# Entry to the ternary convolution: another order of buffers, five for attention outputs, one for transformed rows, and half 1's scales and chain ahead of half 0's transform

## The chip, the cores and the metric

The kernel runs on one core of a Trainium2 chip. The metric is the device time of one execution in microseconds (us), as the median of several runs. The engines named below are TensorE (PE, matrix multiply), VectorE (DVE), ScalarE (ACT), GpSimd (POOL) and SyncE (SP, which here only issues transfers). Each engine works through its own instructions in their order and waits for the others by semaphores.

## The reference

Four layers follow each other on an image batch x of shape (4, 256, 64, 64), each as x = x + layer(groupnorm(x)) with 32 groups. They are an axial attention, a ternary 3x3 convolution, a block of binary convolutions and a convolution with generated weights. The change lies where the first gives way to the second.

```python
def _L0_conv_ref(x, w_qkv, ...):      # axial attention along one image axis
    ...
    sim = jax.nn.softmax(sim, axis=3)
    attn = jnp.einsum('ngij,ngcj->ngci', sim, v)
    attn_e = jnp.einsum('ngij,cij->ngci', sim, v_emb)
    out = jnp.concatenate([attn, attn_e], axis=-1)
    out = out.reshape(N, 2 * OUT_C, W)
    out = _bn(out, bn3_gamma, bn3_beta, axes=(0, 2), ch_axis=1)
    out = out.reshape(B, H, OUT_C, 2, W).sum(axis=-2)
    return out.transpose(0, 2, 1, 3)

def _L1_conv_ref(x, weight, alpha, bias):
    w_t = _ternize_ste(weight, THRESHOLD) * alpha
    out = jax.lax.conv_general_dilated(x, w_t, window_strides=(1, 1), padding=[(1, 1), (1, 1)], ...)
    return out + bias[None, :, None, None]

x = x + _L0_conv_ref(_gn(x), ...)
x = x + _L1_conv_ref(_gn(x), L1_conv_weight, L1_conv_alpha, L1_conv_bias)
x = x + _L2_conv_ref(_gn(x), ...)
x = x + _L3_conv_ref(_gn(x), ...)
```

The batch norm at the end of the attention needs the mean and variance over the whole batch, so the attention's outputs are stored first and scaled afterwards, when the next layer loads them. The group norm at the start of the convolution needs the sums of one whole image.

## The kernel before, in words

**The end of the attention.** It works in eight units, one for each image b and each half th of the 256 channels (half 0 of all four images, then half 1). For a unit, the softmax numbers of the tile pt are multiplied with the values (matmul on L945, eight pieces k) and with the embedded values (matmul on L970). DVE scales each piece out of PSUM into an SBUF tile: o0 (L954) for the first kind, o1 (L977, two pieces to a tile) for the second. The tile's statistics are taken (L959, L984), and ACT's queue issues its store to the tensors at_d in memory (L960, L985). The scale rb is copied from PSUM by ACT on L938. The tiles o0 and o1 have two buffers each.

**The convolution** lies in the function from_scores, in one with-block that opens its pools on L1227. An image is cut into four quarters q of 16 rows, and each quarter lies in two halves t of 128 channels. These steps are made of it:

- load(b, t, q), L1258: makes the row tile dx from the input x (the load is the helper's L145) and the two attention outputs, a1 (two loads on L1270, scaled by ACT on L1273, added by DVE on L1275) and a0 (a load of L145, multiplied and added by DVE on L1278, which also yields the sum). ACT squares the result into a junk tile for the sum of squares (L1256). The scales come from value_norm(t, two), L786, which ends the attention's batch norm for a half; before the change it is called for half 0 earlier, and for half 1 inside load(0, 1, 0).
- norm(b, ts), L1283: from the sums of an image's half to the group norm's factors: a chain of small operations on DVE (L1105 to L1110, L1292, L117 to L128 of the helpers, L1297 to L1300), three small matmuls (L115, L125, L126) and a square root on ACT.
- transform(b, t, q), L1303: ACT writes the normed rows into a padded tile (L1316), DVE makes the transformed rows dv of them (L1318, L1322, L1323), ACT casts dv into dh (L1328) and DVE takes the rest dl = dv - dh (L1329).
- chunk(b, q, co), L1334: 48 matmuls (L1351) of dh and dl of both halves with the weights d_u, for output half co; then the bias and the sums (L1366 to L1370), the addition to dx (L1375), another square, and stores to x2_d and, for co = 1, to z_d by POOL's queue (L1380, L1382).

The weights d_u are loaded by load_weights (L1246). The first chunk takes all products of half 0 before those of half 1 (by_tile). The driver at the end of the block loads five quarters ahead of the chunk at work and transforms one quarter ahead.

**What sets order and place.** The program is written to a scheduler that gives each engine an instruction order from the written order and its priorities (a with-block tc.high_priority() puts its contents ahead). The pools are laid out one after another in the order in which they are opened, over memory that the attention's tiles use as well. An instruction that writes into memory waits until the earlier tile on that memory was last read. In before the pools for the sums (tag st in the pool s), for the junk (in the pool o), for half 1's first row tile, for d_u1 and for half 1's dv lie over the attention's tile pt, which is read until the last matmul of L970.

**The next layer**, of binary convolutions, starts by loading x2_d (L1538) and its weights e_k (L1495) through SP's queue. ACT takes signs into the padded tile e_pad (L1549), DVE transforms them into e_tr (L1436), and PE multiplies them on L1447. Before these, the norm of the last image is ended and one small matmul (pbad) counts bad values.

Of the kernel before, what the change touches and what calls it, by code (L numbers as in the profile page):

```python
# [9 lines left out]
F32 = mybir.dt.float32  # L10
F32R = mybir.dt.float32r
BF16 = mybir.dt.bfloat16
# [6 lines left out]
P = 128  # L19
B = 4  # L20
C = 256
HW = 4096
# [19 lines left out]
def network(ctx: ExitStack, tc, x, wqkv, relm, relt, relw, relv, counts, masks, vecs, rowv, ab, w1, l2w1, l2w2, l3w, mats, out):  # L42
# [45 lines left out]
    def pool(stack, name, bufs=1, space=None, side=None):  # L88
        kw = {"space": space} if space is not None else {}
        return stack.enter_context(tc.tile_pool(name=name, bufs=bufs, side=side, reuse_waits="tile", **kw))  # L90
# [3 lines left out]
    def fresh(base):  # L94
        uid[0] += 1
        return f"{base}_{uid[0]}"
# [45 lines left out]
    def load_shuffled(dst, src, t):  # L142

        rows = src.rearrange("(two i) f -> i two f", two=2)[64 * t : 64 * t + 64]
        nc.sync.dma_start(out=dst, in_=rows)  # L145
# [20 lines left out]
    with ExitStack() as ph:  # L166
# [9 lines left out]
        pst = pool(ph, "a_pst", 1, PSUM)  # L176
# [102 lines left out]
        for b in range(B):  # L279
            xs, gm, rs = ready  # L280
# [129 lines left out]
    with ExitStack() as ph:  # L410
# [3 lines left out]
        op = pool(ph, "b_o", 2)  # L414
# [22 lines left out]
        for t in range(2):  # L437
            v = small(sp, [P, 2])
# [196 lines left out]
        for b in range(B):  # L635
            for gp in range(GP):
                j = 4 * b + gp // 2
                if j == 2 and gp % 2 == 0:
                    load_sums()
                q = qs[j]  # L640
# [103 lines left out]
    def from_scores(general, keep):  # L744
# [41 lines left out]
        def value_norm(th, two, psp, tag):  # L786


            mv3 = small(keep, [P, 2])
            nc.vector.bn_aggr(mv3, st3[:, th, two].rearrange("p k s -> p (k s)"))  # L790
            var, gam = mv3[:, 1:2], vec[:, V_BN3G + 2 * th + two : V_BN3G + 2 * th + two + 1]
            if two == 0:

                sv = s1[:, 2 + th : 3 + th]
                nc.vector.tensor_tensor(var, var, sv, ALU.mult)
                nc.vector.tensor_tensor(var, var, sv, ALU.mult)
                g = small(keep, [P, 1])
                nc.vector.tensor_tensor(g, gam, sv, ALU.mult)
                gam = g
            prm = small(keep, [P, 2])  # L800
            r = inv_std(keep, var, BN_EPS, [P, 1])
            nc.vector.tensor_tensor(prm[:, 0:1], r, gam, ALU.mult)
            nc.vector.tensor_tensor(prm[:, 1:2], mv3[:, 0:1], prm[:, 0:1], ALU.mult)
            beta = vec[:, V_BN3B + 2 * th + two : V_BN3B + 2 * th + two + 1]
            nc.vector.tensor_tensor(prm[:, 1:2], beta, prm[:, 1:2], ALU.subtract)
            ps = psp.tile([P, 2], F32, name=f"pprm{th}{two}", tag=tag)
            nc.tensor.matmul(ps, lhsT=mt[:, M_SHUF, :], rhs=prm, start=True, stop=True)
            res = small(keep, [P, 2])
            nc.vector.tensor_copy(res, ps)
            return res  # L810
# [415 lines left out]

        with ExitStack() as ph:  # L1227
            ps_ = {
                k: pool(ph, f"d_{k}", {"a": 3, "o": 2}.get(k, 1))
                for k in "x2 x3 a x4 x5 x0 x6 p0 v0 h00 l00 u0 u1 x1 o s v1 h10 l10 h11 l11 x7 x8 x9 p1 x10 x11 h01 l01".split()  # L1230
            }
            ap_, op, sp = ps_["a"], ps_["o"], ps_["s"]
            wide = pool(ph, "d_ps3", 1, PSUM)
# [3 lines left out]

            pads = [ps_[f"p{t}"].tile([P, 18, 66], F32, name=f"d_pad{t}", tag="pad") for t in range(2)]
            u = [ps_[f"u{t}"].tile([P, 3, 4, C], F32R, name=f"d_u{t}", tag="u") for t in range(2)]
            for t in range(2):  # L1240
                nc.vector.memset(pads[t][:, :, 0], 0.0)
                nc.vector.memset(pads[t][:, :, 65], 0.0)

            def load_weights(t):
                for dx in range(3):
                    nc.sync.dma_start(out=u[t][:, dx].bitcast(F32), in_=u1_d[:, t, dx])  # L1246
# [3 lines left out]
            def row_of(b, t, q):  # L1250
                xs[b, t, q] = ps_[f"x{2 * ((4 * b + q) % 6) + t}"].tile([P, HW // 4], F32, name=f"dx_{b}_{t}_{q}", tag="x")
                return xs[b, t, q]

            def square(src, out):
                junk = op.tile([P, HW // 4], BF16, name=fresh("dj"), tag="j", bufs=1)
                nc.scalar.activation(junk, src, AF.Square, accum_out=out)  # L1256

            def load(b, t, q):  # L1258

                if (b, t) not in sums:  # L1260
                    sums[b, t] = sp.tile([P, 4, 2], F32, name=f"dst_{b}_{t}", tag=f"st{t}", bufs=2)
                xt = row_of(b, t, q)
                load_shuffled(xt, x[b][:, bass.ts(q, HW // 4)], t)
                if b == 0 and t == 1 and q == 0:
                    for two in range(2):
                        prs[t, two] = value_norm(t, two, pst, "pst")
                a = ap_.tile([P, HW // 4], F32, name=f"a1_{b}_{t}_{q}", tag="a")
                for two in range(2):
                    src = at_d[1][b][t * P + 64 * two : t * P + 64 * two + 64].rearrange("i (k f) -> i k f", k=4)
                    nc.sync.dma_start(  # L1270
                        out=a[two:P:2].rearrange("p (k f) -> p k f", k=4), in_=src[:, :, bass.ts(q, 256)]
                    )
                nc.scalar.activation(a, a, AF.Copy, scale=prs[t, 1][:, 0:1])  # L1273
                xv = xt.rearrange("p (n k i) -> p n k i", k=4, i=16)
                nc.vector.tensor_tensor(xv, a.rearrange("p (k n i) -> p n k i", k=4, i=16), xv, ALU.add)  # L1275
                a = ap_.tile([P, HW // 4], F32, name=f"a0_{b}_{t}_{q}", tag="a")
                load_shuffled(a, at_d[0][b][bass.ts(t, P), bass.ts(q, HW // 4)], 0)
                nc.vector.scalar_tensor_tensor(  # L1278
                    xt, a, prs[t, 0][:, 0:1], xt, ALU.mult, ALU.add, accum_out=sums[b, t][:, q, 0:1]
                )  # L1280
                square(xt, sums[b, t][:, q, 1:2])
# [21 lines left out]
            def transform(b, t, q):  # L1303


                nb, ra = norms[b, t]
                pad = pads[t]
                if q in (0, 3):
                    nc.vector.memset(pad[:, 0 if q == 0 else 17, :], 0.0)
                parts = [(xs[b, t, q].rearrange("p (h w) -> p h w", w=64), slice(1, 17))]  # L1310
                if q > 0:
                    parts.append((xs[b, t, q - 1][:, 15 * 64 :].rearrange("p (h w) -> p h w", w=64), slice(0, 1)))
                if q < 3:
                    parts.append((xs[b, t, q + 1][:, 0:64].rearrange("p (h w) -> p h w", w=64), slice(17, 18)))
                for src, rows in parts:
                    nc.scalar.activation(pad[:, rows, 1:65], src, AF.Identity, bias=nb, scale=ra)  # L1316
                v = ps_[f"v{t}"].tile([P, 4, 8, 66], F32, name=f"dv_{b}_{t}_{q}", tag="v")
                nc.vector.tensor_tensor(  # L1318
                    v[:, 0:4:3].rearrange("p k q w -> p q k w"), pad[:, 0:16].rearrange("p (q k) w -> p q k w", k=2),
                    pad[:, 2:18].rearrange("p (q k) w -> p q k w", k=2), ALU.subtract,  # L1320
                )
                nc.vector.tensor_tensor(v[:, 1], pad[:, 1:17:2], pad[:, 2:18:2], ALU.add)  # L1322
                nc.vector.tensor_tensor(v[:, 2], pad[:, 2:18:2], pad[:, 1:17:2], ALU.subtract)  # L1323
                hi, lo = (
                    ps_[f"{k}{(4 * b + q) % 2}{t}"].tile([P, 4, 8, 66], F32R, name=f"d{k}_{b}_{t}_{q}", tag="tr")
                    for k in "hl"
                )
                nc.scalar.copy(hi, v)  # L1328
                nc.vector.tensor_tensor(lo, v, hi, ALU.subtract)  # L1329
                vs[b, t, q] = hi, lo  # L1330
# [59 lines left out]
            for q in range(4):  # L1390
                load(0, 0, q)
            load_weights(0)
            with tc.high_priority():
                norm(0, slice(0, 1))
            transform(0, 0, 0)
            for q in range(4):
                load(0, 1, q)
            load_weights(1)
            norm(0, slice(1, 2))
            transform(0, 1, 0)  # L1400
            for t in range(2):
                load(1, t, 0)
            for b in range(B):
                for q in range(4):
                    nxt = (b, q + 1) if q < 3 else (b + 1, 0)
                    far = divmod(4 * b + q + 5, 4)
                    for co in range(2):
                        if nxt[0] < B:
                            transform(nxt[0], co, nxt[1])
                        chunk(b, q, co, b == q == co == 0)  # L1410
                        if far[0] < B:
                            load(far[0], co, far[1])
                    if far[0] < B and far[1] == 3:
                        norm(far[0], slice(0, 2))
# [472 lines left out]
```

## Time and profile before

| | us |
|---|---|
| three runs | 2746.36, 2769.91, 2764.95 |
| median | 2764.95 |
| profiled execution | 2755.02 |
| its span | 2753.1 |
| granted clock of TensorE in it, mean | 0.936 of full speed |
| busy in the span: PE, DVE, ACT, POOL | 2399.8, 1978.8, 1202.4, 105.2 |
| last matmul of the attention (L970) ends at | 1463.1 |
| first matmul of the convolution (L1351) | 1489.81 |
| last matmul of the convolution ends at | 1890.9 |
| first matmul of the next layer (L1447) | 1906.59 |

A table by stretch gives busy time of each engine between two times of the span. A list of waits gives, for an engine and a line, how long it stood idle just before an instruction of that line and what ended the wait. A time line gives runs of equal instructions of one engine with the start, the busy time, the line, the operation, and in brackets the idle time before and what ended it. In names, the buffer numbers are left out: dx stands for all row tiles, a for both kinds of attention outputs, sm for small tiles.

### The profile page before, as it was taken

To read this page: it belongs to the slowest core of one execution; us is meant where nothing else is said; L and a number is where in the kernel's file an instruction comes from. 1 tells how busy PE (TensorE), PEld (TensorE's weight loads), DVE (VectorE), ACT (ScalarE), POOL (GpSimd) and SP (SyncE) were. 2 spreads that over 40 slices of the span, in tenths; PEclk is the share of its full clock that TensorE was granted. 3 is DMA by queue.
4 is the path that set the end of the run, shared out by engine and by line. 5 is a ranking of instruction groups with operands and counts; after the bars stand their busy time and mean duration, and the time that the engine had idled before them with its cause. 6 is when DMAs were issued, how large, how long until landed. Compare 5 with 4: busy or idle time off the path is not lost. (4 is left out here: it accounts for less than half of the span.)

```text
span 2753.1 us, 78131 instructions
## 1 busy us (share of the span) xinstructions
PE 2399.8 (87%) x34632; PEld 1582.9 (57%) x34632; DVE 1978.8 (72%) x3372; ACT 1202.4 (44%) x1984; POOL 105.2 (4%) x201
## 2 busy tenths in 40 slices
PE   7999788888998788888773999997979859999998
PEld 4666555656666566667663777775545424444443
DVE  6665788878675466666567999885878877867742
ACT  3555245545555644454444665553458411110100
POOL 0000100000001000000000000000000000000000
PEclk9999899999999899988986999998989979999999
DMA  6866366656656877777777655415347742424110
GB/s 234 269 197 193 92 185 178 162 162 188 160 148 146 238 260 243 263 246 250 250 234 237 211 191 195 159 67 191 127 146 261 279 157 92 144 101 138 46 44 34
DMA packets 287995, 489.86 MB, mean 178 GB/s; under 512 B 32736, under 2 KB 149088, under 8 KB 274848
## 3 DMA queue, kind: packets, MB, share of 16 engines
q1 hardware_dynamic: 224992, 359.52, 42.9%
q10 hardware_dynamic: 48256, 58.73, 6.2%
q0 software_dynamic: 14400, 66.53, 6.2%
q8 instruction: 273, 4.47, 0.7%
q14 instruction: 74, 0.61, 0.1%
HBM read 281.46 MB, written 203.23 MB: 176 GB/s over the span
## 5 line engine op out<-in xcount | busy, mean ns | idle before, releaser
L1066 PE MATMUL gc<-gtr,g_u 128*128 128x512 f32 x1152 | 504.4, 600 | 13.6 <-DVE pc_o L1459 6.9
L1066 PEld LDWEIGHTS gc<-gtr,g_u 128*128 128x128 f32 x1152 | 219.6, 192 | 290.1 <-issue 270.8
L512 DVE STREAM_TRANSPOSE t<-pd 128x1024 f32<-128x1024 f32 x256 | 304.5, 1228 | 93.4 <-PE pd L505 92.3
L505 PE MATMUL pd<-rm,qb 64*32 64x256 f32 x8192 | 312.6, 396 | 44.2 <-DVE t L512 34.7
L1447 PE MATMUL pc<-e_tr,e_k 128*64 128x512 bf16 x2304 | 264.3, 390 | 24.3 <-DVE e_tr L1436 17.9
L532 ACT ACTIVATE o<-pq 128x512 f32<-128x512 f32 x256 | 150.4, 593 | 274.2 <-PE pq L526 270.1
L505 PEld LDWEIGHTS pd<-rm,qb 64*32 64x32 f32 x8192 | 172.9, 109 | 138.1 <-DVE t L512 60.5
L1351 PE MATMUL dc<-dh,d_u 128*128 128x512 f32 x768 | 229.6, 407 | 15.6 <-ACT dh L1328 15.6
L907 ACT ACTIVATE pt<-pt,sm 128x512 f32<-128x512 f32 x256 | 162.6, 709 | 177.0 <-DVE pt L877 136.6
L1351 PE MATMUL dc<-dl,d_u 128*128 128x512 f32 x768 | 227.8, 404 | 4.1 <-DVE dl L1329 4.1
L1447 PEld LDWEIGHTS <-e_k 128*64 128x64 bf16 x2304 | 150.1, 112 | 135.4 <-issue 31.6
L526 PEld LDWEIGHTS pq<-t,t 64*64 64x64 f32 x8192 | 146.4, 139 | 85.5 <-issue 70.8
L526 PE MATMUL pq<-t,t 64*64 64x64 f32 x8192 | 168.0, 226 | 27.2 <-issue 22.1
L1351 PEld LDWEIGHTS dc<-dh,d_u 128*128 128x128 f32 x768 | 146.0, 191 | 54.5 <-ACT dh L1328 16.1
L877 DVE TENSOR_TENSOR pt<-e_False,si_False 128x1024 f32<-128x1024 f32 x128 | 151.5, 1215 | 33.7 <-PE e_False L867 28.7
L1351 PEld LDWEIGHTS dc<-dl,d_u 128*128 128x128 f32 x768 | 144.3, 189 | 44.8 <-DVE dl L1329 6.7
L1084 ACT COPY gc_c<-gc 128x512 f32<-128x512 f32 x32 | 18.6, 581 | 344.6 <-PE gc L1066 344.6
L867 PE MATMUL e_False<-qc_False,rw 32*128 32x256 f32 x1024 | 132.6, 481 | 30.8 <-DVE pt L877 15.7
L538 ACT ACTIVATE sq<-o 128x1024 bf16<-128x1024 f32 x128 | 135.3, 1057 | 4.0
L293 PE MATMUL po<-xg,wt 128*128 128x512 f32 x256 | 122.4, 618 | 6.7 <-DVE st L300 5.1
L308 PE MATMUL pv<-wt,xg 128*128 128x256 f32 x512 | 121.3, 385 | 0.0
L970 PE MATMUL pe_False<-pt,ve 128*32 128x64 f32 x4096 | 91.9, 245 | 31.5 <-issue 24.6
(401 smaller groups left out, 3597.0 us busy)
## 6 DMA issues: line engine op xcount, KB each, us to landing
si_False<-qk_d SPq DMA_DIRECT2D x64, 1024.0 KB
qk_d<-o SPq DMA_DIRECT2D x496, 128.0 KB
x<-x_d SPq DMA_DIRECT2D x32, 1056.0 KB
xa<-in_x SPq DMA_DIRECT2D x16, 1024.0 KB
vt_d<-vs ACTq DMA_DIRECT2D x32, 512.0 KB
q_d<-qs SPq DMA_DIRECT2D x64, 256.0 KB
qb<-q_d SPq DMA_DIRECT2D x128, 128.0 KB
qc_False<-q_d SPq DMA_DIRECT2D x64, 256.0 KB
```

Source lines behind the costliest of these rows:

```text
L293: nc.tensor.matmul(psf, lhsT=wt[:, t, bass.ts(o, P)], rhs=xg[:, t, :], start=(t == 0), stop=(t == 1))
L505: nc.tensor.matmul(pds[t][32 * c : 32 * c + 32, m].rearrange("p j k -> p (j k)"), lhsT=q[rows, 2 * (gp % 2) + g, a, 32 * nb : 32 * nb + 32 ...
L512: nc.vector.transpose(ts[t][:, :, 32 * jh : 32 * jh + 32].rearrange("p a j b -> p j a b"), pds[t].rearrange("p m j k -> p j m k"),)
L526: nc.tensor.matmul(ps[nb][64 * g : 64 * g + 64, m, :], lhsT=ts[1][rows, n // 2, :, n % 2], rhs=ts[0][rows, n // 2, :, n % 2], start=True, ...
L532: nc.scalar.activation(o[:, :, n : n + 8, :], ps[nb].rearrange("p n (a b) -> p a n b", b=2), AF.Copy, accum_out=acc[:, nb, gp, col : col + 1],
L538: nc.scalar.activation(junk, part, AF.Square, accum_out=acc[:, 2, gp, col : col + 1])
L867: nc.tensor.matmul(es[x_ // 2][:, x_ % 2, :, :, par], lhsT=rw[rows, 63 - i : 127 - i].rearrange("p j r -> p (j r)"), rhs=q[rows, :, par, k ...
L877: nc.vector.tensor_tensor(dst, e, src, ALU.add)
L907: nc.scalar.activation(s, s, AF.Exp, scale=s2q[:, gp : gp + 1])
L1066: nc.tensor.matmul(ms[k], lhsT=u[t][:, dx, k, bass.ts(co, P)], rhs=vs[t][:, k, :, dx : dx + 64], start=(first and dx == 0), stop=(last and ...
L1351: nc.tensor.matmul(at[k], lhsT=u[t][:, dx, k, bass.ts(co, P)], rhs=v[:, k, :, dx : dx + 64], start=(first and p_ == 0 and dx == 0), stop=( ...
L1447: nc.tensor.matmul(m[64 * g : 64 * g + 64], lhsT=parts[:, g, i, k, dx, :], rhs=vs[g][:, k, 8 * (q % 2) : 8 * (q % 2) + 8, dx : dx + 64], s ...
```

## The change

All edits are in the block of the convolution.

- Its pools are opened in another order, so every tile of the block lies elsewhere. The pool a has five buffers instead of three. The two pools v0 and v1 for the transformed rows of the two halves become one pool v. The junk tile gets a pool j of its own, which comes with s, the sums, right after v.
- The row loads of dx are split from load into load_x, and for half 1 of image 0 they are written ahead of the norm of half 0. The clearing of a padded tile's edge columns becomes a function for one half, clear(t).
- The value norms and loads of half 1 of image 0 are written after the norm of half 0 and ahead of transform(0, 0, 0), with high priority; norm, clearing and transform of half 1 have high priority too.
- The first loads of image 1 are written after the first chunk instead of before it.

```diff
             ps_ = {
-                k: pool(ph, f"d_{k}", {"a": 3, "o": 2}.get(k, 1))
-                for k in "x2 x3 a x4 x5 x0 x6 p0 v0 h00 l00 u0 u1 x1 o s v1 h10 l10 h11 l11 x7 x8 x9 p1 x10 x11 h01 l01".split()
+                k: pool(ph, f"d_{k}", {"a": 5, "o": 2}.get(k, 1))
+                for k in "a x0 x2 x4 x6 x1 x3 x5 x7 p0 v s j u0 h00 l00 u1 o p1 h10 l10 h11 l11 x8 x9 x10 x11 h01 l01".split()
             }
...
-            for t in range(2):
+
+            def clear(t):
                 nc.vector.memset(pads[t][:, :, 0], 0.0)
                 nc.vector.memset(pads[t][:, :, 65], 0.0)
...
             def square(src, out):
-                junk = op.tile([P, HW // 4], BF16, name=fresh("dj"), tag="j", bufs=1)
+                junk = ps_["j"].tile([P, HW // 4], BF16, name=fresh("dj"), tag="j")
                 nc.scalar.activation(junk, src, AF.Square, accum_out=out)
+
+            def load_x(b, t, q):
+                load_shuffled(row_of(b, t, q), x[b][:, bass.ts(q, HW // 4)], t)
 
             def load(b, t, q):
...
-                xt = row_of(b, t, q)
-                load_shuffled(xt, x[b][:, bass.ts(q, HW // 4)], t)
-                if b == 0 and t == 1 and q == 0:
-                    for two in range(2):
-                        prs[t, two] = value_norm(t, two, pst, "pst")
+                if (b, t, q) not in xs:
+                    load_x(b, t, q)
+                xt = xs[b, t, q]
...
-                v = ps_[f"v{t}"].tile([P, 4, 8, 66], F32, name=f"dv_{b}_{t}_{q}", tag="v")
+                v = ps_["v"].tile([P, 4, 8, 66], F32, name=f"dv_{b}_{t}_{q}", tag="v")
...
             load_weights(0)
+            for q in range(4):
+                load_x(0, 1, q)
             with tc.high_priority():
                 norm(0, slice(0, 1))
+                for two in range(2):
+                    prs[1, two] = value_norm(1, two, pst, "pst")
+                for q in range(4):
+                    load(0, 1, q)
+            load_weights(1)
+            clear(0)
             transform(0, 0, 0)
-            for q in range(4):
-                load(0, 1, q)
-            load_weights(1)
-            norm(0, slice(1, 2))
-            transform(0, 1, 0)
-            for t in range(2):
-                load(1, t, 0)
+            with tc.high_priority():
+                norm(0, slice(1, 2))
+                clear(1)
+                transform(0, 1, 0)
...
                         chunk(b, q, co, b == q == co == 0)
+                        if b == q == co == 0:
+                            for t in range(2):
+                                load(1, t, 0)
```

## The prediction

> **What bounds the kernel now.** I first read the busy time by stretch over the whole ternary convolution, to see where TensorE (PE) is not full. Columns: start:end, length, busy time and instructions of PE, PE's weight loads, DVE, ACT, POOL, then granted clock, DMA share, GB/s.
>
> ```profile
> 1425.00:1463.00 38.00, 23.41 (x921) 21.89 (x919) 20.99 (x36) 4.34 (x4) 0.93 (x2) 0.78 0.65 215
> 1463.00:1490.00 27.00, 3.11 (x22) 2.63 (x12) 20.71 (x62) 13.94 (x21) 0.00 (x0) 0.56 0.74 243
> 1490.00:1520.00 30.00, 11.72 (x39) 8.87 (x40) 25.74 (x44) 21.25 (x29) 0.00 (x0) 0.67 0.70 223
> 1520.00:1570.00 50.00, 50.00 (x202) 39.01 (x201) 47.03 (x55) 32.03 (x40) 3.27 (x6) 0.96 0.66 214
> ...
> 1720.00:1770.00 50.00, 50.00 (x210) 39.26 (x210) 48.98 (x66) 31.46 (x40) 3.70 (x7) 1.00 0.58 199
> ```
>
> From 1520 on PE is full and a faster convolution is not on offer. What can be gained lies before 1520: PE has 14.6 idle us of 38 at the end of attention and 42.2 of 57 at the entry; DVE is the busy engine there. The waits of the two stretches (engine, line, for what: us in total, times, longest) say which:
>
> ```profile
> DVE o_False L954 <- DMA at_d<-o_False: 13.5, 3, 6.0
> ```
> ```profile
> PE pst L115 <- DVE sm L1292: 24.6, 2, 15.9
> ...
> ACT dj L1256 <- DVE dx L1278: 22.8, 4, 17.7
> ...
> PE dc L1351 <- ACT dh L1328: 15.6, 2, 8.5
> ```
>
> Then the time line of PE and DVE. The last attention matmul ends at 1463.1 (called T from here).
>
> ```profile
> 1489.81 2.93 PE L1351 MATMUL dc<-dh,d_u 128*128 128x512 f32 x6 [7.14 <-ACT dh L1328]
> ...
> 1507.55 0.58 PE L115 MATMUL pst<-sm,mt 128*128 128x1 f32 x2 [8.63 <-DVE sm L1292]
> ...
> 1518.96 2.93 PE L1351 MATMUL dc<-dh,d_u 128*128 128x512 f32 x6 [8.48 <-ACT dh L1328]
> ```
> ```profile
> 1466.72 1.27 DVE L1278 SCALAR_TENSOR_TENSOR dx<-a,sm,dx 128x1024 f32<-128x1024 f32 x1
> ...
> 1504.11 1.28 DVE L1278 SCALAR_TENSOR_TENSOR dx<-a,sm,dx 128x1024 f32<-128x1024 f32 x1
> ```
>
> Half 0's convolution starts at T+26.7, does 30 matmuls, and PE then waits for half 1 until T+55.9. The last sum of half 1 (second DVE line) comes at 1504; behind it stand square, norm chain, pad, dv, dh: 13.7 us in series. The third place is the way out, where the next layer starts:
>
> ```profile
> 1867.22 0.33 SPq L1495 DMA_DIRECT2D e_k<-bk_d  x1
> 1868.05 21.71 SPq L1538 DMA_DIRECT2D x<-x_d  x4
> ```
> ```profile
> 1905.73 4.42 DVE L1436 TENSOR_TENSOR e_tr<-e_pad 128x1056 bf16<-128x1056 bf16 x7 [3.52 <-DMA z_d<-dx]
> ```
>
> DVE's first e_tr of the last set waits for a store of the convolution's own dx: its memory lies under the new tile. PE is idle 5.18 us for it and starts at 1906.59.
>
> **What the Trainium skill says.** "Perfetto Trace Analysis", section Optimization Strategy: look for gaps on the limiting engine and find what would release them; repeated bubbles can mean too few buffers. The trace agrees: the 13.5 us on L954 are waits for a buffer. "DMA: Bandwidth & Descriptors", section Issuing engines are not separate DMA queues: loads and stores of all queues share 16 engines. The trace agrees: the stores behind the 5.96 us wait left while 1.5 MB of dx loads ran (299 GB/s in 1430:1435). "TensorE: Matmul & The Clock Gate", section What's actually happening: a PE that was idle runs at half clock for a few us. The clock of 0.56 after T agrees, and 6 matmuls took 2.93 us (later 3 take 0.88).
>
> **The change part by part.** The profiled execution took 2755.02 (span 2753.1); the median of the three runs is 2764.95, 9.9 above. I sum against 2755.02.
>
> *Placement and loads (five a, s and j early, u0, dx of half 1).* Before, sums, junk and half 1's dx lie over the attention's last score tile pt, so the additions on L1278 cannot run before T. Afterwards they lie over tiles that are free from about 1444, and the built order of DVE puts two of the four additions of half 0 ahead of the last attention evictions. Two go before T: 2 x 1.28 = 2.6 us. The fifth a buffer frees the fourth: its a1 was issued only at 1468 and its addition waited until 1474.4, against 1471.3 with nothing to wait for: 3.1 us.
>
> *Half 1 first.* Before, transform (0,0,1) and the dv after it stand between half 1's additions on DVE: dv 2.65, dl 2.35, dv 2.65 = 7.7 us. After, half 1's loads, sums and chain come ahead of them. Together 2.6 + 3.1 + 7.7 = 13.4 on the path to half 1. Built up from T: evictions and statistics left over and half 0's sums to T+7.5, square and chain to T+14 (chain 4.9 before), four times 1.22 + 1.28 of half 1 with half 0's dv (2.65) and value norms to T+28, dl 2.35, chain 6.2 to T+36.6, pad 1.25, dv 2.65, dh 1.95: half 1's convolution at T+42.5, before T+55.9. **13.4 us.** Half 0's own start stays at about T+27: half 1's TTs now stand ahead of its dv. That costs nothing, because PE only waits for half 1 afterwards.
>
> *The end of attention.* The dx loads of half 0 move to about 1405, into a stretch with 3 GB/s (1410:1415), and d_u0's three loads to attention's second unit. Behind them stand the scores' loads; their engine waits (L877, 33.7 us over 128) were on PE for 28.7, so that is covered. Fewer loads lie ahead of the stores on L954, worth up to 7 us of 13.5. Against it, half 1's dx and first a1 (2.5 MB, 7.2 us at the 346 GB/s of 1420:1425) now run at 1444 to 1456 beside the o1 stores; ACT's scale before the second rb copy delays one eviction by 0.45. Bounds: 7 gained, 2 lost. I take **4**.
>
> *Paid back.* The 7.7 us of DVE work put off comes next. When half 1 starts, PE has 63 matmuls at 0.239 (15 us, a few at half clock), DVE needs 16 to 22 us for what the next chunk wants. Bounds: 0 to 7 lost; I take **4.5**.
>
> *The way out.* In the new placement that e_tr lies over dl, done long before, and x2's loads stand ahead of e_k's on SP. PE can start when the norm matmul pbad (1901.2) is done: 5.2 us earlier, or a little more or less with the loads: 3 to 7, I take **5.5**.
>
> *One v instead of two.* dv of the next transform now cannot precede dl of the last. On DVE the built order puts 2.4 to 4.0 us of other work between dv and dl for images 0 to 2, against ACT's 1.95 for dh, so dl finds dh ready. For image 3 it is 0 to 1.7, but DVE has 35.3 of 50 there (1820:1870). I take 0, bound 1 us each over the last 8: 8 us. Memsets by half (0.07 each) and queues POOL (stores, unmoved): 0; PE covers them.
>
> Sum: 13.4 + 4 - 4.5 + 5.5 = **18.4 us faster**: 2736.6 for a run like the profiled one, 2746.5 at the median.
>
> **Rivals.**
> 1. *Gains add and nothing is paid back.* 13.4 + 7 + 7 = 27 and PE's clock warm a little earlier (2 to 3): 30 us, 2735 at the median. For: DVE 47 of 50 leaves some room and PE's first matmuls are slow. Against: the put-off work is real.
> 2. *The collision eats it.* Half 1's loads hold the o1 stores, T comes 2 late, DVE pays 7: 13.4 - 2 - 7 + 3 = 7 us, 2757. For: DMA share 0.89 in 1445:1450. Also here: the change does not do what it says, if half 0's chain waits for half 1's loads on DVE: half 1's start moves by less than 13.
> 3. *Slower: single v makes DVE the bound.* If dl must wait for dh on the in-order DVE, each of the 30 later transforms loses s. DVE's slack is 3.9 of 50, so 0.9 us of a chunk's 11.5 (48 x 0.239); the loss is 30 x (s - 0.9), and it beats the gain from s = 1.5 on. With s = 2.3 (whole dh and its hand-off): 42 - 18 = 24 slower, 2789. For: 48.98 of 50 in 1720:1770. Against: the filler above.
>
> **Chances.** Forecast (12 to 25 gained) 0.50, rival 1 0.25, rival 2 0.17, rival 3 0.08. About 1% (27.6 us) is what this kernel's measurement tells from no change. Faster by more: rival 1's larger part and the tail of the forecast, 0.27; slower by more: rival 3's worse part, 0.05; within: 0.68. The range runs from rival 1 with a fast sample (10 under) to a rival 2 that gains nothing: 2724 to 2766.
>
> **What would show it.** The changed profile should have: two L1278 additions before the last attention matmul; T near 1459; half 1's restart of PE 42 to 43 after T; a PE wait of 2 to 5 us in the 25 us after it; no wait of e_tr on z_d, first pc matmul some 10 to 11 after the convolution's last. Wrong would be: waits of dl (L1329) on ACT dh that add up in 1520:1890, PE under 48 of 50 there, or waits on L954 as long as now.

## The result and the profile after

The changed kernel takes 2744.7 us in the median of 22 runs against 2756.66 of the kernel before, a ratio of 0.9953 (95% interval 0.9938 to 0.9967): 12.0 us faster between the medians and 13.0 by the ratio. The sum had said 18.4. The profiled execution has a span of 2733.4 us, 19.7 less than the one before, but that is more than the change gave. The first copy of rb, early in the attention, starts at 933.5 in it and at 941.1 before: the two executions stand 7.6 us apart where both kernels have run the same code. So all marks below are counted from the end of the last copy of rb, late in the attention ("rb", 1429.5 before, 1420.2 after) or from T, the end of the attention's last matmul.

The same table by stretch as before the change, of the changed kernel:

```profile
1425.00:1463.00 38.00, 17.57 (x704) 16.27 (x704) 26.87 (x50) 7.24 (x10) 0.00 (x0) 0.70 0.75 255
1463.00:1490.00 27.00, 9.08 (x31) 7.10 (x32) 20.92 (x62) 16.46 (x23) 0.00 (x0) 0.54 0.89 303
1490.00:1520.00 30.00, 25.92 (x102) 19.59 (x101) 28.31 (x36) 22.29 (x28) 0.63 (x1) 0.94 0.53 164
1520.00:1570.00 50.00, 49.44 (x207) 38.56 (x206) 46.78 (x68) 29.43 (x39) 4.23 (x8) 1.00 0.63 212
1570.00:1620.00 50.00, 43.75 (x173) 33.55 (x172) 40.57 (x88) 31.70 (x43) 2.11 (x4) 0.93 0.54 179
```

The rows have the same bounds as before the change, but the changed kernel is 9.3 us ahead at rb. Counted from T, PE does 28.4 us of the next 57 where it did 14.8 (the changed kernel, then the one before):

```profile
1456.40:1513.40 57.00, 28.40 (x103) 21.52 (x104) 49.23 (x105) 33.84 (x47) 0.00 (x0) 0.69 0.74 241
```
```profile
1463.10:1520.10 57.00, 14.83 (x52) 11.60 (x50) 46.45 (x104) 35.29 (x49) 0.00 (x0) 0.62 0.72 232
```

Later PE has a hole of 6 us in 1570:1620 that the kernel before did not have there. The time line of PE and of its waits in the changed kernel (L1353 is the convolution's matmul, before L1351):

```profile
1483.60 2.93 PE L1353 MATMUL dc<-dh,d_u 128*128 128x512 f32 x6 [13.87 <-ACT dh L1330]
...
1497.99 2.70 PE L1353 MATMUL dc<-dh,d_u 128*128 128x512 f32 x6 [4.07 <-ACT dh L1330]
```

With T at 1456.4, half 0 starts at T+27.2 (before T+26.7) and half 1 at T+41.6 (before T+55.9). The waits of the attention's end:

```profile
DVE o_False L954 <- DMA at_d<-o_False: 7.2, 3, 3.9
DVE o_False L977 <- DMA at_d<-o_False: 5.9, 1, 5.9
```

Together 13.1 us, where one line had 13.5: they went from o0's stores to one of o1's. The way out, on PE:

```profile
1887.97 0.19 PE L1430 MATMUL pbad<-mt,sm 128*1 128x1 f32 x2 [0.32 <-DVE sm L128]
1888.09 12.19 PE L1457 MATMUL pc<-e_tr,e_k 128*64 128x512 bf16 x98
```

The next layer starts right behind pbad, 9.1 us after the convolution's last matmul (1879.0) instead of 15.6.

Four marks carry the whole comparison, in us: from rb to T, from rb to half 1's restart, from there to the convolution's last matmul (the stretch), and from that to the next layer's first matmul (the way out). All kernels that ran, with the ratio to the kernel before on the same chip:

| kernel | rb to T | rb to restart | stretch | way out | sum | ratio (interval) |
|---|---|---|---|---|---|---|
| before | 33.6 | 89.5 | 371.9 | 15.6 | 477.1 | 1 |
| after | 36.2 | 77.8 | 381.0 | 9.1 | 467.9 | 0.9953 (0.9938 to 0.9967) |
| after_again | 34.1 | 74.5 | 378.0 | 9.1 | 461.5 | 0.9964 (0.9949 to 0.9980) |
| placement_only | 39.5 | 80.9 | 379.6 | 9.1 | 469.6 | 0.9968 (0.9953 to 0.9982) |
| order_only | 33.8 | 90.1 | 371.7 | 16.7 | 478.5 | 1.0000 (0.9986 to 1.0015) |
| aft_a3 | 33.7 | 83.5 | 378.3 | 9.1 | 470.9 | 0.9985 (0.9969 to 1.0000) |
| aft_a4 | 35.9 | 79.8 | 380.9 | 13.4 | 474.1 | 0.9971 (0.9955 to 0.9987) |
| bef_one_v | 34.1 | 89.6 | 380.0 | 11.7 | 481.4 | 1.0016 (1.0000 to 1.0032) |
| aft_a4_two_v | 32.3 | 78.8 | 373.1 | 12.6 | 464.5 | 0.9968 (0.9953 to 0.9983) |
| bef_way_out | 32.6 | 88.4 | 371.3 | 11.5 | 471.3 | 0.9983 (0.9968 to 0.9997) |
| aft_rows_later | 35.1 | 77.4 | 378.9 | 9.1 | 465.4 | 0.9957 (0.9936 to 0.9977) |
| tail_alone | 25.2 | 89.5 | 381.7 | 15.2 | 486.3 | one run, 2768.56 us |
| two_v_held | 34.3 | 78.2 | 373.5 | 9.1 | 460.8 | 0.9949 (0.9927 to 0.9971) |
| two_v_later | 35.9 | 78.7 | 373.6 | 9.1 | 461.3 | 0.9941 (0.9919 to 0.9962) |

The sum is the second to fourth mark. Marks are read to 0.1 us, so a sum or a difference can be off by one in its last digit. How far the marks repeat was tested by the changed kernel once more:

> The changed kernel once more, on the chip of these runs, to see how far the marks repeat and to have its ratio beside the next one's: from the last rb copy to T 36 (35 to 37), to half 1's restart 78, the stretch 381, the way out 9.1, each within 1.5 us; ratio to the kernel before 0.9945 to 0.9970.

It held for the way out and the ratio only; T came 2.1 us earlier, the restart 3.3 earlier, and the stretch was 3.0 shorter. A difference of up to about three us in one mark of one execution is therefore not read as an effect; the two executions gain 9.2 and 15.6 in the sum, on either side of the 12 to 13 of the runs.

### The profile page after: what moved, and what is told of

Its sections match the earlier page's. It is cut to its first block, busy times and chain, and to the rows that moved or that the text cites. A ratio compares the mean times of both kernels' runs of the same rounds, so it can differ in the third digit from the quotient of the medians.

```text
span 2733.4 us, 78106 instructions
## 1 busy us (share of the span) xinstructions
PE 2393.6 (88%) x34632; PEld 1574.3 (58%) x34632; DVE 1978.0 (72%) x3372; ACT 1202.9 (44%) x1984; POOL 105.2 (4%) x201
## 4 chain that ended last, share of the span: by engine, by line
issue 36%; PE 34%; DVE 13%; DMA 9%; ACT 5%; SPq 2%; POOL 1%; DVEq 0%; POOLq 0%; ACTq 0%
PE dc L1353 10%; PE pd L505 5%; PE po L293 3%; PE pv L308 3%; DMA at_d<-o_False 3%; PE pq L526 3%; PE e_False L867 2%; DMA x<-x_d 2%; DVE pt L877 2%; PE pa_False L945 1%; PE den_False L918 1%; PE pr_False L936 1%; PE pe_False L970 1%; DMA qc_False<-q_d 1%; DVE e_tr L1446 1%
## 5 line engine op out<-in xcount | busy, mean ns | idle before, releaser
L505 PE MATMUL pd<-rm,qb 64*32 64x256 f32 x8192 | 306.1, 389 | 41.4 <-DVE t L512 33.3
L1353 PE MATMUL dc<-dh,d_u 128*128 128x512 f32 x768 | 229.7, 410 | 22.5 <-ACT dh L1330 21.4
L1353 PE MATMUL dc<-dl,d_u 128*128 128x512 f32 x768 | 226.6, 405 | 1.9 <-DVE dl L1331 1.8
L1353 PEld LDWEIGHTS dc<-dh,d_u 128*128 128x128 f32 x768 | 146.3, 192 | 63.4 <-ACT dh L1330 22.9
L877 DVE TENSOR_TENSOR pt<-e_False,si_False 128x1024 f32<-128x1024 f32 x128 | 151.5, 1215 | 31.9 <-PE e_False L867 26.8
L1353 PEld LDWEIGHTS dc<-dl,d_u 128*128 128x128 f32 x768 | 144.8, 190 | 43.2 <-DVE dl L1331 4.7
L867 PE MATMUL e_False<-qc_False,rw 32*128 32x256 f32 x1024 | 130.7, 476 | 26.5 <-DVE pt L877 13.6
```

What stands on the lines that cost most here:

```text
L505: nc.tensor.matmul(pds[t][32 * c : 32 * c + 32, m].rearrange("p j k -> p (j k)"), lhsT=q[rows, 2 * (gp % 2) + g, a, 32 * nb : 32 * nb + 32 ...
L867: nc.tensor.matmul(es[x_ // 2][:, x_ % 2, :, :, par], lhsT=rw[rows, 63 - i : 127 - i].rearrange("p j r -> p (j r)"), rhs=q[rows, :, par, k ...
L877: nc.vector.tensor_tensor(dst, e, src, ALU.add)
L1353: nc.tensor.matmul(at[k], lhsT=u[t][:, dx, k, bass.ts(co, P)], rhs=v[:, k, :, dx : dx + 64], start=(first and p_ == 0 and dx == 0), stop=( ...
```

## Experiments: what brought half 1 forward

The change does two things at once, so each was run alone. Placement alone keeps the old written order:

```diff
 # before.py with the pools of after
-{"a": 3, "o": 2} ... "x2 x3 a x4 x5 x0 x6 p0 v0 h00 ..."
+{"a": 5, "o": 2} ... "a x0 x2 x4 x6 x1 x3 x5 x7 p0 v s j u0 ..."
-v = ps_[f"v{t}"].tile(...)
+v = ps_["v"].tile(...)
 ...                            # and the junk tile in the pool j
```

> The changed kernel's pools (order, five a, one v, sums and junk early) with the old written order of loads, norms and transforms. Theory: placement gives the two early sums and the free a buffer, and the single v also holds back half 0's second transform; half 1's restart at T+44 to T+50, the convolution's stretch after it at 380 (single v), the way out at 9 to 12. Rival: the restart at T+42 as in the changed kernel, so that the rewritten order adds nothing; or at T+54 or later, so that placement does nothing for half 1 and the order does all.

The restart came at T+41.4, as the rival said, but T itself was late (39.5 after rb), so from rb it was 80.9: 8.6 of the 11.7 to 15.0 us that the whole change gives there. Half 0's matmuls start at T+19.1 in this run, 7 to 8 us earlier than in the two executions of the changed kernel, and half 1 restarts no earlier for it. The order alone is the changed text with the old pool line, two v and the junk back in o:

> The changed kernel's written order with the old pools: three a, sums and junk and half 1's first rows over the attention's last tile, two v. Theory: without placement half 1's sums cannot start before T and wait for a buffers, and with a second v half 0's next transform may still slip in ahead; half 1's restart at T+47 to T+53, the stretch at 372, the way out at 15.6: 3 to 8 us faster than before. Rival: the order alone gives the whole step, the restart at T+42 to T+44, and placement was not needed; then it beats the changed kernel at the entry and by 9 us in the stretch.

```diff
 # after.py with the pools of before
-{"a": 5, "o": 2} ... "a x0 x2 x4 x6 x1 x3 x5 x7 p0 v s j u0 ..."
+{"a": 3, "o": 2} ... "x2 x3 a x4 x5 x0 x6 p0 v0 h00 ..."
-v = ps_["v"].tile(...)
+v = ps_[f"v{t}"].tile(...)
 ...                            # and the junk tile in the pool o
```

Nothing came of it: 90.1 from rb, T+56.3, ratio 1.0000. Both the expectation (T+47 to T+53) and its rival fell. Without the placement the order is worth nothing. That it adds something to the placement is not shown: from rb the whole change is 3 to 6 us ahead of placement_only (77.8 and 74.5 against 80.9), but nearly all of that lies before T in one execution; from T the restarts are 41.6 and 40.4 against 41.4, and the intervals of the three ratios cover each other.

The prediction had put 7.7 us of the step down to half 0's next transform, which stood between half 1's additions on DVE. Another run removed it from there by accident. The kernel before with a single v:

```diff
-v = ps_[f"v{t}"].tile([P, 4, 8, 66], F32, ...)
+v = ps_["v0"].tile([P, 4, 8, 66], F32, ...)    # and no pool v1
```

> The kernel before with one buffer for the transformed rows instead of two, everything else in its old order (what lies behind v1 moves down by one such tile). In the kernel before, VectorE waited 3.1 us for ACT's cast (dl on L1329 for dh) from half 1's restart to the convolution's end, and that stretch took 371.9 us; in the changed kernel it waited 13.2 us there and the stretch took 381.0, with 9.1 us of PE time lost. Theory S (the single v costs them): here VectorE's wait for the cast rises to 10 us or more and the stretch grows by 5 to 9 us, so the kernel becomes slower by about 5 (0.2%), less what the moved tiles give at the way out. Theory D (the work put off at the entry costs them, v is free): the stretch stays within 2 us of 372 and the waits for the cast below 6.

Here the second transform must wait for half 1's first, so that between half 1's additions DVE has only the first dv and dl left, as in placement_only; yet the restart stayed at 89.6. DVE's time line of bef_one_v between T and the restart shows what it did instead:

```profile
1488.07 1.28 DVE L1278 SCALAR_TENSOR_TENSOR dx<-a,sm,dx 128x1024 f32<-128x1024 f32 x1
...
1491.67 1.23 DVE L1275 TENSOR_TENSOR dx<-a,dx 128x1024 f32<-128x1024 f32 x1 [2.32 <-ACT a L1273]
...
1496.54 1.23 DVE L1275 TENSOR_TENSOR dx<-a,dx 128x1024 f32<-128x1024 f32 x1 [2.32 <-ACT a L1273]
```

SP's queue in the same stretch:

```profile
1484.77 1.18 SPq L1270 DMA_DIRECT2D a<-at_d  x2
...
1489.38 1.18 SPq L1270 DMA_DIRECT2D a<-at_d  x2
...
1494.25 1.20 SPq L1270 DMA_DIRECT2D a<-at_d  x2
```

and ACT, with a quarter's square (L1256) and the next quarter's scale (L1273):

```profile
1489.45 1.06 ACT L1256 ACTIVATE dj<-dx 128x1024 bf16<-128x1024 f32 x1 [1.68 <-DVE dx L1278]
...
1490.50 1.13 ACT L1273 ACTIVATE a<-a,sm 128x1024 f32<-128x1024 f32 x1
1494.32 1.06 ACT L1256 ACTIVATE dj<-dx 128x1024 bf16<-128x1024 f32 x1 [2.68 <-DVE dx L1278]
...
1495.37 1.13 ACT L1273 ACTIVATE a<-a,sm 128x1024 f32<-128x1024 f32 x1
```

An addition ends at 1489.35 and frees a buffer, and the next pair of loads leaves at 1489.38. The scale at 1490.50 does not wait for a load: the pair that it scales had left at 1484.77, and its last transfer had ended at 1488.96. It stands behind the square of the quarter before in ACT's order, and that square waits for the addition. So one quarter is square, scale and two additions, one after the other: 1.05, 1.13, 1.23 and 1.28 us, 4.87 from one square to the next. The work that the prediction wanted out of the way had only filled DVE's waits in this loop.

The number of a buffers comes in through how many scales run ahead of half 1's first square: three with five buffers (two in tail_alone, described below), two with four, one in the next run, with three. In the kernel before there are two, but the first of them starts only at T+19.8 (T+13.6 in the changed kernel). No run changed ACT's order alone, so this path is read from the traces. The test changes the number of buffers:

```diff
-{"a": 5, ...}  "a x0 x2 ... l11 x8 x9 x10 x11 h01 l01"
+{"a": 3, ...}  "a x8 x9 x0 x2 ... l11 x10 x11 h01 l01"   # the rest stays in place
```

> The changed kernel with three buffers for attention outputs, as before the change; x8 and x9 fill the place of the other two, so every other tile of the entry lies where the changed kernel has it. From the last rb copy to half 1's restart it took 89.5 us in the kernel before, 77.8 in the changed one, 79.8 with four. Theory B (the loop of load, scale, add and free over three buffers sets half 1's sums, and the work between them on VectorE only fills its waits): 85 to 90 us, with waits of the addition on L1277 for the scaled a that add up to 5 or more between T and the restart. Rival O (the order of VectorE's work is what gained): 81 or less. The stretch afterwards stays at 380 (one v), the way out at 9.

83.5 from rb, between the two theories (85 to 90, and 81 or less); the waits for a, in DVE's list between T and the restart, are there, if shorter than foreseen (the longest of the first line, 2.3, is again a scale behind a square on ACT):

```profile
DVE dx L1277 <- ACT a L1275: 3.8, 4, 2.3
DVE dx L1280 <- DMA a<-at_d: 2.9, 2, 2.5
```

The 2.5 of the second line is a wait for a load, at half 0's last addition; half 1's first scale comes at T+17.8 instead of T+13.6. So part of what the buffers bring lies there, and part in the scales.

So two more buffers are worth 5.7 to 9.0 us (between the runs on one chip 8.2 by the medians, 2752.92 and 2744.71, and 5.8 by the ratios), and 6.0 come from the rest of the change with three (89.5 to 83.5). How these 6.0 divide between the place of the sums and the order was not tested. With four, `"a": 5` made `"a": 4` and nothing else:

> The changed kernel with four buffers for attention outputs instead of five; a control for the next run, in which memory for the second v is made by this. Theory: the fourth buffer already frees a1 of the fourth quarter; half 1's restart stays within 1.5 us of T+41.6 and the time within 3 us of the changed kernel. Rival: the fifth buffer is what lets half 1's first outputs come early; half 1's restart is later by 2 us or more. The stretch from half 1's restart to the convolution's end stays at about 381 in either case.

79.8, and T+43.9 as the rival said: 3.7 us come with the first of the two buffers. What was not foreseen is the way out, 13.4. With every tile moved by 4 KB, SP's loads of x2_d (L1548) wait 12.4 us for a store of a dx tile to z_d; in the changed kernel they wait for no such store. So another late row tile seems to lie under a tile of the next layer.

## Experiments: what was paid back

The stretch is 371.3 to 371.9 in the three kernels with the old pools and two v, 373.1 to 373.6 in the three new layouts with two v, and 378.0 to 381.7 in all eight executions with one. bef_one_v shows it in the kernel before, as theory S said: 8.1 us longer, with 12.3 us of waits of dl for the cast instead of 3.1, and a ratio of 1.0016 (1.0000 to 1.0032) although its way out was 3.9 shorter. The reverse, four a and a second v at the end of the layout, against the control aft_a4:

```diff
-"a ... p0 v s j ... h01 l01"
+"a ... p0 v0 s j ... h01 l01 v1"
-v = ps_["v"].tile(...)
+v = ps_[f"v{t}"].tile(...)
```

> The changed kernel with four buffers for attention outputs and two for the transformed rows, the second at the end of the layout. Theory S (single v costs the 9 us): VectorE's wait for the cast falls from 13 to about 3 us and the stretch from half 1's restart to the convolution's end from 381 to 372 to 375, 6 to 9 us faster than the control with four buffers and one v. Theory D (the work put off costs them): PE still loses 6 to 9 us in the 100 us after half 1's restart, and the time is within 2 us of the control.

The stretch fell by 7.8 and the waits for the cast from 12.4 to 3.3, as theory S said. The runs do not show it by themselves: the sums of the marks are 9.6 us apart, the medians of 22 runs each only 3.3, and 0.9968 and 0.9971 have intervals that cover each other. The waits for the cast are not the whole mechanism, though. DVE's waits for the cast, in the changed kernel from the restart on and in the kernel before:

```profile
DVE dl L1331 <- ACT dh L1330: 13.2, 14, 2.5
```
```profile
DVE dl L1329 <- ACT dh L1328: 3.1, 3, 2.2
```

Of the 13.2, 9.3 lie after 1700, where PE waits only 1.6. PE's hole is at the step from image 0 to image 1. In all eight executions with one v PE waits 4.5 to 6.2 us in the first quarter of image 1, in the six with two v 0 to 2.9; its 96 matmuls take 30.1 to 31.9 us against 23.5 to 27.1. PE in the changed kernel:

```profile
1588.10 1.70 PE L1353 MATMUL dc<-dh,d_u 128*128 128x512 f32 x6 [1.86 <-ACT dh L1330]
1590.17 0.99 PE L1353 MATMUL dc<-dh,d_u 128*128 128x512 f32 x3 [0.37 <-DVE dc_o L1372]
1592.43 2.41 PE L1353 MATMUL dc<-dl,d_u 128*128 128x512 f32 x9 [1.28 <-DVE dl L1331]
1597.34 0.58 PE L115 MATMUL pst<-mv,mt 128*128 128x2 f32 x2 [2.50 <-DVE bias L1339]
...
1599.07 4.19 PE L1353 MATMUL dc<-dh,d_u 128*128 128x512 f32 x9
```

DVE there, in the changed kernel (the last piece of a dv, then its dl, for one half and the other):

```profile
1585.32 0.70 DVE L1325 TENSOR_TENSOR dv<-d_pad 128x528 f32<-128x528 f32 x1
...
1590.03 2.35 DVE L1331 TENSOR_TENSOR dl<-dv,dh 128x2112 fp32r<-128x2112 f32 x1
...
1595.23 0.70 DVE L1325 TENSOR_TENSOR dv<-d_pad 128x528 f32<-128x528 f32 x1
...
1598.49 2.35 DVE L1331 TENSOR_TENSOR dl<-dv,dh 128x2112 fp32r<-128x2112 f32 x1
```

and in two_v_held, which has two v and is described below:

```profile
1590.79 0.70 DVE L1325 TENSOR_TENSOR dv<-d_pad 128x528 f32<-128x528 f32 x1
...
1593.20 0.70 DVE L1325 TENSOR_TENSOR dv<-d_pad 128x528 f32<-128x528 f32 x1
1593.82 2.35 DVE L1331 TENSOR_TENSOR dl<-dv,dh 128x2112 fp32r<-128x2112 f32 x1
...
1596.69 2.35 DVE L1331 TENSOR_TENSOR dl<-dv,dh 128x2112 fp32r<-128x2112 f32 x1
```

The first transform of a new image waits for that image's norm, so no lead is left there. With two v DVE makes both dv, 2.4 us apart, while ACT casts the first; from the end of the first dv to the end of the second dl it takes 7.6 us. With one v the second dv stands behind the first dl, and an addition, two steps of a finished chunk and 1.7 us of idle time lie between the two dv as well, and it takes 14.8. The list of waits does not name this: the second dv waits in DVE's own order.

## Experiments: the two ends

The attention's end was to become 4 us shorter. First the early loads of half 1's rows were taken away:

```diff
             load_weights(0)
-            for q in range(4):
-                load_x(0, 1, q)
```

> The changed kernel without the separate, early loads of half 1's rows of the input; they are issued with half 1's attention outputs instead. In the changed kernel one eviction (L977) waited 5.9 us for a store of o1 while these 2 MB were moving, and from the last copy of rb to T it took 37.2 us against 34.6 in the kernel before. Theory C (the loads collide with the stores): the wait on L977 falls below 2 us and T comes 3 to 5 us earlier from the last rb copy; half 1's rows land later, so its restart comes at T+43 to T+47, and the sum is within 3 us of the changed kernel. Rival: the stores collide with half 0's own outputs, not with these loads: the waits on L954 and L977 stay at about 13 us together and T where it was, and the kernel is 2 to 5 us slower by the late rows.

(The 37.2 and 34.6 of the expectation are counted from the start of the rb copy, 1.0 earlier than the marks of the table.) The wait on L977 fell from 5.9 to 2.6, that on L954 rose from 7.2 to 9.4, and T came at 35.1, inside what the changed kernel itself does (36.2 and 34.1). Theory C fell and the rival's waits stayed (12.0 together); these loads matter little. Then everything of the convolution was moved away from it, by placing a and half 1's rows over the attention's last tile (and leaving out the same early loads):

```diff
-"a x0 x2 x4 x6 x1 x3 x5 x7 p0 v s j u0 h00 l00 u1 o p1 h10 l10 h11 l11 x8 x9 x10 x11 h01 l01"
+"x8 x9 x10 x11 x0 x2 x4 x6 p1 h01 l01 p0 v s j u0 h00 l00 u1 o a x1 x3 x5 x7 h10 l10 h11 l11"
```

> How long the attention's end takes when nothing of the convolution runs beside it: the a tiles and half 1's row tiles lie over the attention's last tile, so that their loads and all additions wait for T; half 0's and image 1's rows come before 1415. From the last rb copy to T, 33.6 us in the kernel before and 36.2 in the changed one. Theory C (loads and additions of the convolution hold the evictions and their stores): 26 to 30 us, the waits of L954 and L977 for stores below 5 together. Rival (the attention's own evictions and stores with two buffers each take this long): 32 or more, and the waits stay at 8 or more. The time as a whole says nothing here; the entry comes later by 10 or more.

Theory C held for the whole: 25.2 us, just under its 26 to 30, in one execution. The stretch from rb to T by busy times, in tail_alone, in the kernel before and in the changed one:

```profile
1432.60:1457.80 25.20, 17.05 (x849) 15.47 (x841) 19.50 (x41) 1.53 (x3) 0.00 (x0) 0.93 0.37 137
```
```profile
1429.50:1463.10 33.60, 19.01 (x838) 17.54 (x832) 19.43 (x33) 2.32 (x3) 0.00 (x0) 0.75 0.70 236
```
```profile
1420.20:1456.40 36.20, 20.48 (x847) 18.83 (x837) 22.98 (x41) 6.72 (x8) 0.00 (x0) 0.78 0.70 233
```

DMA goes from a share of 0.37 to 0.70, and the evictions' waits for stores from 2.3 to 13. The convolution's early work costs the attention 8 to 11 us in either kernel. Loads and additions were moved away together; in the kernel before DVE is busy as long as here (19.4 and 19.5 us), so there it is not the additions' own time. The change moved which loads lie there, not how many, and added 3.6 us of DVE work.

For the way out, two pools changed places in the kernel before, and nothing else:

```diff
-"... u0 u1 x1 o s v1 h10 l10 h11 l11 x7 x8 ..."
+"... u0 u1 x7 o s v1 h10 l10 h11 l11 x1 x8 ..."
```

> The kernel before with the pools x7 and x1 exchanged and nothing else: half 1's last row tile of the last image no longer lies under the next layer's first e_tr tile. Theory P (that overlap is what the changed kernel's way out gained by): PE's first L1447 matmul comes 10 to 12 us after the convolution's last matmul instead of 15.6, and the kernel is 4 to 5 us faster. Rival L (the gain came from x2's loads going ahead of e_k's on SP): the way out stays at 13 to 16 us, and the time within 2 us.

11.5 instead of 15.6, 0.9983 (4.7 us): the overlap under e_tr gave 4.1 of the 6.5. The rest, 2.4, can be read and was not tested alone. In the kernel before, ACT's last square stood behind a sign that waited for an x2 load:

```profile
1894.71 2.06 ACT L1549 ACTIVATE e_pad<-x,sm 128x2112 bf16<-128x2112 f32 x1 [3.92 <-DMA x<-x_d]
1896.67 1.04 ACT L1256 ACTIVATE dj<-dx 128x1024 bf16<-128x1024 f32 x1
```

In the changed kernel that sign is done at 1880.4, and the square follows its addition at once (1882.14).

## Experiments: a better version

If one v does good at the entry (it holds half 0's second transform back) and harm later, then that one tile can be held back with two v. x8 takes the place of the fifth a, so the entry's tiles stay where they are:

```diff
-{"a": 5, ...}  "a x0 x2 ... p0 v s j ... l11 x8 x9 x10 x11 h01 l01"
+{"a": 4, ...}  "a x8 x0 x2 ... p0 v0 s j ... l11 x9 x10 x11 h01 l01 v1"
-v = ps_["v"].tile(...)
+v = ps_["v1" if (b, t, q) == (0, 0, 1) else f"v{t}"].tile(...)
```

> The changed kernel with four a and two v, laid out so that row tiles, sums, u0 and dh stay where the changed kernel has them (x8 takes the fifth a's place, v1 goes to the end). Half 0's second transform alone takes v1, so that it must wait for half 1's first, as the single v made it wait. Theory S+H (the single v did two things: it held back half 0's second transform at the entry, for good, and made VectorE wait for the cast later, for ill): half 1's restart at T+41 to T+44, the stretch at 372 to 375, the way out at 9 to 11, 6 to 9 us faster than the changed kernel, 0.9925 to 0.9945 of the kernel before. Rival: the stretch grows back to 378 or more because of the work put off at the entry.

Restart 78.2, stretch 373.5, way out 9.1: 460.8 in all, 16.3 less than before, ratio 0.9949, just outside the 0.9925 to 0.9945 that were expected. That holding the transform back does good is not shown: aft_a4_two_v, which does not hold it back, has a restart of 78.8 and a stretch of 373.1, and only its way out (12.6) is longer. Without the early row loads:

> The version with four a, two v and half 0's second transform held back, and without the early loads of half 1's rows. Those loads cost 1.1 us at the attention's end in one comparison. Theory: from the last rb copy to half 1's restart 76 to 78, the stretch 373, the way out 9: 458 to 460 from the last rb copy to the next layer, 8 to 10 less than the changed kernel; ratio 0.993 to 0.995. Rival: with four a the late rows arrive too late and the restart is at 80 or more, so that nothing is left over the version with early rows (460.8).

461.3, no better by the marks; 0.9941. On that chip the changed kernel had 0.9964 and a median of 2744.71 (22 runs) against 2739.6 here (6 runs; two_v_held had 9). Both versions have the lowest ratios of the study, but their intervals reach into that of the changed kernel, so that they beat it is likely and not shown. They do beat the kernel before.

## Why the prediction was right and where it was not

- **The time and its sign.** 2746.5 was forecast, with faster by 18.4; 2744.7 was measured, faster by 12 to 13, because the kernel before has its median at 2756.66 over 22 runs, not at 2764.95. That the time itself came within 2 us is luck: the gain was put 5 to 6 us too high, and the median that it was taken from was 8.3 too high. Within 1% had the highest chance and came.
- **Half 1's restart, 13.4 after T: right in size (14.3 and 15.5), wrong in its parts.** The step that failed is "transform (0,0,1) and the dv after it stand between half 1's additions on DVE ... 7.7 us". They filled waits of DVE in a loop that goes through ACT: bef_one_v removed them and gained nothing, order_only gained nothing, and the buffers, counted at 3.1, bring 5.7 to 9.0. Half 1's four scales on ACT start between T+19.8 and T+37.0 in the kernel before, between T+13.6 and T+24.2 in the changed one and, with three a, between T+17.8 and T+33.1.
- **Half 0's start near T+27:** held (27.2 and 26.0), and it cost nothing: placement_only starts half 0 at T+19.1 and restarts half 1 at T+41.4.
- **The end of attention, 4 gained:** 2.6 and 0.5 lost, none by the repeat's spread. "Fewer loads lie ahead of the stores on L954, worth up to 7" was true of L954 (13.5 to 7.2), and a new wait of 5.9 for an o1 store took it back, near the bound of 2 lost. That half 1's row loads make this wait is not borne out: without them T came at 35.1. tail_alone shows that the convolution's early work costs it 8 to 11 in either kernel.
- **Paid back, 4.5, and one v, 0:** the two terms lost 9.1 and 6.1 together, against 4.5 in the sum, and the split was wrong. The work put off costs 1.6 at most (two_v_held 373.5 against 371.9); one v costs 4.5 to 8.1. The failing step is "On DVE the built order puts 2.4 to 4.0 us of other work between dv and dl ... so dl finds dh ready". dl did wait, 13.2 us in all; and the step did not ask what stands behind dl: the other half's dv, at an image's first quarter. Nor was PE full everywhere after 1520, as the prediction has it: the kernel before itself waits 2.9 us at the step from image 1 to image 2 (47.09 of 50 in 1670:1720, a row that its table leaves out). Rival 3 had the right place and too many of them: not 30 transforms, but one change of image.
- **The way out, 5.5:** 6.5, by the named overlap for 4.1.
- **The signs.** Two of half 0's four final additions (L1280 in the changed kernel) do lie before T, and no e_tr waits for z_d. But two of the three signs of being wrong came too: waits of dl (13.2 us), and PE at 43.75 of 50 in 1570:1620. And the PE wait of 2 to 5 us in the 25 us after the restart did not come; PE runs without a wait there.

The terms that came out worse than summed (the end, the payback) leave 9.2 and 15.6 in the two traces, around the 12 to 13 of the runs.

## What to carry to other kernels

Before work is moved out of an engine's queue, look at whether it fills waits there: take the filler away in thought and see what the engine would then wait for, here a scale that stands behind a square on another engine. When two tiles share one buffer on an in-order engine, look for what now stands behind the reader of the first, at the place where the lead is smallest; a list of waits does not show it. And where tiles of two stages share memory, a 4 KB shift can move the start of the next stage by 4 us, so compare the way out of every layout.

## What the runs showed of the hardware

PE lost more here than it waited. From the restart to the last matmul, the list of PE's waits sums to 9.1 us in the changed kernel and to 4.1 in the one before, 5.0 more, while the stretch is 9.1 longer. After the waits at the image change, none of them over 2.5 us but with only six matmuls of two columns between 1594.8 and 1599.1, nine matmuls took 4.19 us (at 1599.07) where three take 0.88 elsewhere. The granted clock was 0.73 in 1595:1600 and 0.59 in 1600:1605. Groups of three at full speed start 0.72 us apart, so nine would take 2.2: by this estimate about 2 of the 4.1 us that the waits leave were lost here, and the rest stays open. Executions of one program spread by 1% (2732.91 to 2760.39 in 22 runs), and from the first rb copy to the last two executions of the changed kernel took 486.7 and 494.0 us; what was compared across executions had to be counted from a mark close by.
